# A two-layer graph kernel: counting steps, zeroing, the split of x and two orders of work are changed together

## The chip, the cores and the metric

One Trainium2 chip, one NeuronCore. The time is the device time of the whole program in microseconds (us). A run gives one time; the figure before is the median of three runs.

## The reference

A graph of 6,250 nodes with 256 features and 100,000 edges sorted by their target. Two layers, each a sum over incoming edges, then two dense products; at the end the input is added and every row is normalised:

```python
def _gin_agg(h, src, dst, eps, n_nodes):
    agg = jax.ops.segment_sum(h[src], dst, num_segments=n_nodes)
    return (1.0 + eps) * h + agg
...
h = _gin_agg(x, src, dst, eps1, n)
h = jax.nn.relu(h @ W1a + b1a)          # 256 -> 512
h = jax.nn.relu(h @ W1b + b1b)          # 512 -> 512
h = _gin_agg(h, src, dst, eps2, n)
h = jax.nn.relu(h @ W2a + b2a)          # 512 -> 512
out = h @ W2b + b2b                     # 512 -> 256
...
x = _layernorm(x + out)
```

The targets are drawn as 6250 u², so the first nodes have very many edges and the last ones few.

## The kernel before

Nodes stand in 49 tiles of 128 rows, edges in 782 chunks of 128. The program runs in three parts: a preparation (edge lists are turned and verified; the result is a flag), layer 1 and layer 2. A set flag sends the program into a slow general path; here it isn't set.

**Two ways of summing.** The edges of the first tiles (tiles 0 to 9 in layer 1, 340 chunks) are *counted*: for every pair of target and source the kernel counts how many edges there are, and the sum over edges becomes a dense product of the matrix of counts with all of x. The other chunks are *gathered*: POOL fetches 128 source rows per chunk by an indirect DMA (L504), and TensorE sums them with a selection matrix (`sums`, L1211; `merge`, L1256; VectorE adds into the tile's accumulator, L1268).

**Counting** (`counting`, `counted_`; layer 1 only). For each chunk VectorE makes `ca`, a one-hot matrix of the low seven bits of the source (L1883; one instruction makes four chunks), and `cb`, a one-hot row of the tile and the target's place in a window of w nodes (L1893). TensorE multiplies them (L1936, `ca` is stationary). 245 *steps* of one to eight chunks run from the last counted chunk down: 31 of one chunk and w = 11, which take two PSUM banks each; 149 of one chunk and w = 7 to 10; 65 of more chunks. After a step ScalarE copies the first w − 1 columns into the 8-bit table `at` (or the 16-bit `at_first`) at a place that a register holds (L1977), and VectorE adds the last column to what stands there (L1985). Before the first such copy both tables are zeroed by ScalarE (`zeroing`, L1912). A step needs a *permit* from a room of `SIDE` = 3 before it asks for its banks, and gives it back after the addition. Steps of one chunk with w ≤ 10 are started two at a time, and such a pair needs both its permits first.

**Products of counts with x** (`first_products`). x is loaded in ranges of four tiles into one buffer `raw`, split into an upper and a lower part (`splitting`, L1696 to L1699), stored as `halves`, and multiplied with the counts in three passes over all 49 tiles (`PASSES`: tiles 9 and 8, tiles 7 to 4, tiles 3 to 0; L1752 converts counts, L1811 multiplies). The first pass takes the split tiles as they come; the others load `halves` again. A pass starts when its tiles have been counted.

**The dense part** (`dense`): transposes (L1334), the first product (L1383), ScalarE's relu (L1393), the second product (L1412), and in layer 1 a store of the result h (L1426).

**Layer 2** gathers rows of h, so its gathers start after the last store of layer 1. Its counted tiles 0 to 7 use the counts kept in DRAM: `second_products` goes over 13 ranges of four tiles from the last to the first (`rs`; the last range, 12, is one tile of 106 rows), with two buffers for rows of h (`xr`, `upper`) and two for each kind of counts (`ci`). For the first two ranges of that order the rows are loaded and halved at the end of layer 1 (`sooner`, `SOONER` = 2).

**The order of work** on each engine is written out by a planner (`Plan`) when the program is built: it runs all of these as processes over rooms of buffers (eight PSUM banks among them) with estimated costs; counting steps ask for TensorE with priority 0, like sums, dense work with 2. On the chip each engine follows its list in order and waits on semaphores.

## Time and profile before

| | us |
|---|---|
| median of three runs | 1537.58 |
| lowest and highest | 1535.27, 1547.84 |
| the profiled execution's own time | 1526.32 |
| its span from the first to the last instruction | 1524.6 |
| mean granted TensorE clock (share of full speed) | 0.935 |
| TensorE busy | 1297.8 (85%) |
| VectorE, ScalarE, POOL busy | 811.6, 618.4, 895.2 |

Preparation ends at about 28 us, layer 1 at about 746 us. A share of busy time is over the whole span; what an edit is worth has to be read in the stretch in which it lies. Instructions are named by engine (PE is TensorE, PEld its weight loads, DVE VectorE, ACT ScalarE, SP the queue that issues most DMAs) and by the line of the kernel.

### The profile page before, as it was taken

The page shows a single profiled execution, that of the slowest core. Times are in us where ns is not written, and L with a number is a line of the kernel's source. Part 1 is how long each engine was busy: PE and PEld are TensorE (multiplying, and loading weights), DVE is VectorE, ACT ScalarE, POOL GpSimd, SP SyncE. Part 2 cuts the span into 40 slices and gives each one's busy share as a digit, 9 for nine tenths or more (in the row PEclk, how much of TensorE's full clock was granted, in tenths as well). Part 3 has the DMA queues.
Part 4 walks back from the last instruction along what each step waited for, and adds up shares of the span by engine and source line. Part 5 has one row for each costly group of instructions (what it writes and reads, how often), then busy time and mean ns, then how long its engine had stood idle before and what let it go on. Part 6 is the DMA issues. An engine that isn't in the chain of part 4 may idle for free.

```text
span 1524.6 us, 20531 instructions
## 1 busy us (share of the span) xinstructions
PE 1297.8 (85%) x6367; PEld 820.3 (54%) x6367; DVE 811.6 (53%) x2122; ACT 618.4 (41%) x1293; POOL 895.2 (59%) x944
## 2 busy tenths in 40 slices
PE   3478978879888899889968999997989999979997
PEld 2135545436554445555545666665556665656665
DVE  5575756655567883113146665764455544534343
ACT  3656556545555434444533423323233323321211
POOL 7565665565666766661256656664666666656640
PEclk7589988989999999999989999999999999999999
DMA  4555666647774436893478767776677877767650
GB/s 122 163 168 177 221 210 201 204 126 228 235 229 127 119 117 197 272 288 106 160 253 303 228 199 255 225 217 213 210 238 245 259 235 234 221 178 210 199 163 27
DMA packets 154445, 304.29 MB, mean 200 GB/s; under 512 B 34606, under 2 KB 69254, under 8 KB 154328
## 3 DMA queue, kind: packets, MB, share of 16 engines
q0 software_dynamic: 59136, 182.25, 39.6%
q1 hardware_dynamic: 87716, 107.04, 21.6%
q10 hardware_dynamic: 7476, 13.60, 2.5%
q8 instruction: 54, 0.88, 0.2%
q14 instruction: 63, 0.52, 0.1%
HBM read 263.18 MB, written 39.63 MB: 199 GB/s over the span
## 4 chain that ended last, share of the span: by engine, by line
PE 69%; DVE 9%; issue 8%; another core or an unknown queue 4%; ACT 4%; DMA 2%; POOL 1%; DVEq 1%; ACTq 1%; SPq 0%; POOLq 0%
PE bank L1383 17%; PE bank L1412 15%; PE bank L1211 11%; PE bank L1648 9%; PE bank L1811 7%; PE bank L1936 4%; PE bank L1256 4%; PE bank L1334 2%; DVE at L1985 1%; DVE cb L1893 1%; DVE acc L1591 1%; DVE acc L1268 1%; DMA xh<-halves 1%; DVE sel L1160 1%
## 5 line engine op out<-in xcount | busy, mean ns | idle before, releaser
L504 POOL DMA_INDIRECT early<-in_x_dram,srcs x442 | 435.9, 986 | 256.4 <-issue 113.0
L504 POOL DMA_INDIRECT early<-h,srcs x238 | 229.7, 965 | 186.5 <-issue 61.5
L504 POOL DMA_INDIRECT late<-h,srcs x236 | 227.2, 963 | 139.8 <-issue 59.1
L1268 DVE SCALAR_TENSOR_TENSOR acc<-bank,mask,acc 128x512 f32<-128x512 f32 (+1 forms) x365 | 210.9, 611 | 80.0 <-PE bank L1256 21.4
L1383 PE MATMUL bank<-zt,wide_w 128*128 128x256 f32 (+2 forms) x832 | 191.4, 387 | 24.5 <-ACT zt L1355 15.3
L1412 PE MATMUL bank<-wide_w,ht 128*128 128x512 f32 (+1 forms) x392 | 188.5, 607 | 3.2 <-DVE xh L1699 3.2
L1383 PEld LDWEIGHTS bank<-zt,wide_w 128*128 128x128 f32 x832 | 159.6, 203 | 55.6 <-ACT zt L1355 17.4
L1211 PE MATMUL bank<-early,sel 128*32 128x256 f32 (+1 forms) x1360 | 157.4, 489 | 30.2 <-issue 20.3
L1648 PE MATMUL bank<-upper,cfs 128*128 128x512 f32 (+1 forms) x392 | 169.4, 432 | 14.6 <-issue 10.9
L1811 PE MATMUL bank<-cf,xh 128*128 128x512 f32 (+2 forms) x588 | 150.2, 389 | 17.1 <-ACT cf L1752 10.2
L1648 PE MATMUL bank<-xr,cfs 128*128 128x512 f32 (+1 forms) x392 | 155.5, 397 | 0.0
L1977 ACT CAST at<-bank 128x250 f32 (+4 forms) x238 | 113.9, 494 | 99.7 <-PE bank L1936 32.6
L1575 ACT CAST cfs<-ci 128x512 fp32r<-128x512 uint8 (+3 forms) x104 | 60.7, 595 | 220.8 <-PE bank L1648 80.1
L1936 PE MATMUL bank<-cb,ca 128*128 128x490 f16 (+7 forms) x371 | 96.2, 340 | 58.6 <-DVE cb L1893 20.0
L1591 DVE TENSOR_TENSOR acc<-bank,acc 128x512 f32<-128x512 f32 x96 | 65.3, 684 | 137.9 <-remote 50.0
L1160 DVE TENSOR_TENSOR sel<-iota,slot 128x256 f32<-128x256 f32 (+3 forms) x109 | 47.6, 436 | 164.8 <-PE bank L1211 122.2
L1811 PEld LDWEIGHTS bank<-cf,xh 128*128 128x128 f32 (+1 forms) x588 | 100.8, 196 | 50.5 <-issue 20.7
L1256 PE MATMUL bank<-split,to 128*128 128x512 f32 (+3 forms) x306 | 89.8, 398 | 38.7 <-DVE split L1246 19.4
L1893 DVE TENSOR_SCALAR cb<-numbers,spot 128x492 f16<-128x492 f16 (+7 forms) x340 | 99.8, 330 | 40.0 <-remote 12.1
L1383 PE MATMUL bank<-zt,narrow_w 128*128 128x256 f32 (+2 forms) x432 | 103.3, 387 | 6.5 <-issue 4.0
L1211 PEld LDWEIGHTS bank<-early,sel 128*32 128x32 f32 x1360 | 40.0, 112 | 127.0 <-issue 107.0
L1412 PEld LDWEIGHTS bank<-wide_w,ht 128*128 128x128 f32 (+1 forms) x392 | 71.2, 193 | 66.7 <-issue 59.6
(150 smaller groups left out, 1702.4 us busy)
## 6 DMA issues: line engine op xcount, KB each, us to landing
xh<-halves SPq DMA_DIRECT2D x48, 512.0 KB
halves<-xh SPq DMA_DIRECT2D x24, 512.0 KB
h<-h1r ACTq DMA_DIRECT2D x48, 256.0 KB
xr<-h SPq DMA_DIRECT2D x12, 1024.0 KB
acc<-h SPq DMA_DIRECT2D x18, 512.0 KB
early<-in_x_dram,srcs POOLq DMA_INDIRECT x442
raw<-in_x_dram SPq DMA_DIRECT2D x12, 512.0 KB
r<-in_x_dram SPq DMA_DIRECT2D x22, 256.0 KB
```

The costliest lines, as they stand in the source:

```text
L504: nc.gpsimd.indirect_dma_start(out=rows_[:, j, :], out_offset=None, in_=table, in_offset=bass.IndirectOffsetOnAxis(ap=srcs[:, c : c + 1], ...
L1211: mm = nc.tensor.matmul(pm[b * SLOTS : (b + 1) * SLOTS], sel[:, c - groups[g][0], :], rows_[:, l, :], start=(c == part[0]), stop=(c == par ...
L1256: nc.tensor.matmul(pu[:, i * width : (i + 1) * width], to[:used], split[:used, l, i * width : (i + 1) * width], start=(l == 0), stop=(l == 1),
L1268: nc.vector.scalar_tensor_tensor(acc[t], pu[:, i * width : (i + 1) * width], mask[:, t - lo[g], g : g + 1], acc[t], op0=ALU.mult, op1=ALU.add,
L1383: nc.tensor.matmul(ph[:, (f - o) * TILES * P : (f - o) * TILES * P + nb], wa[:, k, f * P : (f + 1) * P], zt[:, k, :nb], start=(k == 0), st ...
L1412: nc.tensor.matmul(po[:m], ht[:, f, i * P : i * P + m], wb[:, f, :], start=(f == 0), stop=(f == KH - 1),)
L1591: nc.vector.tensor_tensor(acc[t], bank[token.number][:, :width], acc[t], op=ALU.add)
L1648: nc.tensor.matmul(bank[token.number][:, :width], cf[:m, j, :], of[:m, j, :], start=(j == 0 and of is upper), stop=(j == len(ks) - 1 and o ...
L1811: nc.tensor.matmul(to[:, :c], of, factor, start=(k == 0 and l == 0), stop=last, skip_group_check=True,)
L1893: made = nc.vector.tensor_scalar(token.tile[:, :e], numbers[:, :e], spot[:, c : c + 1], None, op0=ALU.is_equal,)
L1936: mm = nc.tensor.matmul(bank[token[l].number][:, : (k1 - k0) * w], a.tile[:, c % BATCH, :], b.tile[:, k0 * w : k1 * w], start=(j == 0), st ...
L1977: nc.scalar.copy(of[:, k0:k1, UNDER - w + 1 :][:, :, bass.ds(v, w - 1)], ap[:, :, : w - 1],)
```

## The change

- `SIDE` is 4 instead of 3. 
- Zeroing covers only the columns of `at` below the places of the smallest counted targets and above those of the largest (72 and 212 of 1188 bytes per tile, by the constants of the program), and `at_first` as before. The preparation verifies in addition, span by span of steps (`apart`), that each step's window reaches the one before it; one verification over 340 columns shrinks to 8.
- `ca` is laid out with four chunks interleaved: the element of chunk c and column j stands at 4j + c. It is made from a 16-bit copy of the column numbers (`rows_of_`, made once), so both inputs and the output have 16 bits. TensorE's stationary operand is read with a step of four elements.
- x is loaded and split in pairs of tiles with two buffers instead of ranges of four with one, and begins by the planner's clock at 50 instead of 60 us. The small integers of the start use a buffer of `ht` instead of the one of `raw`.
- In layer 1 the last two groups of gathered chunks change places, and the tiles that the last four groups (was three) touch are dense blocks of their own.
- In layer 2 the one-tile range 12 comes last instead of first; so ranges 11 and 10 are the two that are prepared at the end of layer 1.

The diff, cut to its core:

```diff
-SIDE = 3
+SIDE = 4
+SPLIT = 50.0
+RAWS = 2
-ENDING = 3
+ENDING = (4, 3)
...
+        down = list(reversed(range(BEGIN[number - 1], NG)))
+        if number == 1:
+            down[-2:] = reversed(down[-2:])
...
+        before_ = prep.tile([P, NC], F32, name="before_")
+        nc.scalar.copy(before_, cp)
...
-        violated(compare, NC, near, wide_of, op=ALU.is_ge)
+        violated(compare, taken[0][2], near[:, : taken[0][2]], wide_of[:, : taken[0][2]], op=ALU.is_ge)
...
+        def apart(v):
+            for a, b, n, w in taken:
+                if a:
+                    add_compare(
+                        v[:, a - least_n : a - least_n + n], cp[:, a : a + n], -float(w),
+                        before_[:, a - 1 : a].to_broadcast([P, n]), op0=ALU.add, op1=ALU.is_ge,
+                    )
+                if b - a > n:
+                    add_compare(
+                        v[:, a + n - least_n : b - least_n], cp[:, a + n : b], -float(w),
+                        before_[:, a : b - n], op0=ALU.add, op1=ALU.is_ge,
+                    )
...
+        violated(apart, NC - least_n)
...
+        range_order = [*reversed(range(len(ranges) - 1)), len(ranges) - 1]
...
-                raw_room = Tiles(loan, [P, RANGE, width], F32, "raw", 1)
-                scratch = raw_room.take()
+                raw_room = Tiles(loan, [P, PAIR, width], F32, "raw", RAWS)
+                scratch = ht_room.take()
...
-                rs = list(reversed(range(len(ranges))))
+                rs = range_order
...
-                    yield ("rest", 60.0)
-                    for r, ks in enumerate(ranges):
+                    yield ("rest", SPLIT)
+                    landed = []
+                    for q, ks in enumerate(spans):
                         raw = yield ("get", raw_room, 0)
                         in_rows(ks, raw.tile, table)
-                        yield ("rest", LOAD)
-                        for o in range(0, len(ks), PAIR):
-                            two = ks[o : o + PAIR]
...
+                        landed.append(Event(plan))
+                        plan.at(plan.now + LOAD, landed[q].set)
+                        plan.start(parting(q, ks, raw, landed))
+
+                def parting(q, ks, raw, landed):
+                    yield ("until", landed[q])
+                    if q:
+                        yield ("until", parted[q - 1])
...
-                    for i, r in enumerate(reversed(range(len(ranges) - SOONER, len(ranges)))):
+                    for i, r in enumerate(range_order[:SOONER]):
...
-                ca_room = Tiles(loan, [P, BATCH, P], F16, "ca", 4)
+                ca_room = Tiles(loan, [P, P, BATCH], F16, "ca", 4)
+                rows_of_ = loan.tile([P, P, BATCH], F16, name="rows_of_")
...
+                    nc.vector.tensor_copy(
+                        rows_of_, numbers[:, :P].unsqueeze(2).to_broadcast([P, P, BATCH])
+                    )
...
                                 nc.vector.tensor_tensor(
-                                    token.tile[:, :n, :],
-                                    line.unsqueeze(1).to_broadcast([P, n, P]),
-                                    low[:, q * BATCH : q * BATCH + n].unsqueeze(2).to_broadcast(
-                                        [P, n, P]
+                                    token.tile[:, :, :n], rows_of_[:, :, :n],
+                                    low[:, q * BATCH : q * BATCH + n].unsqueeze(1).to_broadcast(
+                                        [P, P, n]
                                     ),
                                     op=ALU.is_equal,
                                 )
...
-                    for k, (of, i, n) in enumerate(
-                        [(at, i, 7) for i in range(0, NT, 7)] + [(at_first, 0, NT)]
-                    ):
-                        some = of[:, i : i + n, :].rearrange("p a b -> p (a b)")
+                    over = (LOW[STEPS[0][0]] - BASE + UNDER) // 4 * 4
+                    under = -(-(HIGH[FINE] - BASE + UNDER + 1) // 4) * 4
+                    for some in (at[:, :, over:], at[:, :, :under], at_first):
                         some = some.bitcast(F32)
...
-                                    a.tile[:, c % BATCH, :], b.tile[:, k0 * w : k1 * w],
+                                    a.tile[:, :, c % BATCH], b.tile[:, k0 * w : k1 * w],
```

## Rows read from the trace of the kernel before

**Rows 1.** First line of the page: span and number of instructions.
```profile
span 1524.6 us, 20531 instructions
```
**Rows 2.** Windows: stretch, length, busy us and instructions per engine, clock, DMA share, GB/s.
```profile
60.00:110.00 50.00, 33.79 (x164) 16.40 (x163) 35.78 (x123) 27.72 (x77) 30.04 (x32) 0.74 0.45 139
110.00:350.00 240.00, 197.48 (x997) 115.69 (x997) 153.97 (x402) 136.09 (x283) 141.87 (x145) 0.90 0.61 190
350.00:600.00 250.00, 221.31 (x1126) 124.85 (x1126) 162.63 (x494) 120.30 (x256) 162.42 (x163) 0.98 0.57 174
600.00:746.00 146.00, 133.80 (x643) 79.45 (x641) 32.13 (x66) 59.46 (x157) 62.26 (x66) 0.99 0.65 208
776.00:1506.00 730.00, 661.28 (x3212) 451.29 (x3213) 386.98 (x770) 228.78 (x446) 435.99 (x452) 0.96 0.70 219
```
**Rows 3.** Windows of the counting matmuls L1936 alone: PE, PEld, clock, DMA, GB/s.
```profile
60.00:110.00 50.00, 14.02 (x56) 5.62 (x55) 0.74 0.45 139
...
120.00:450.00 330.00, 43.79 (x148) 11.49 (x149) 0.93 0.66 205
450.00:580.00 130.00, 34.74 (x159) 13.89 (x157) 0.99 0.41 124
```
**Rows 4.** Timeline (start, us, engine, line), one counting pair and the next.
```profile
206.78 0.59 PE L1936 MATMUL bank<-cb,ca 128*128 128x490 f16 x2
207.19 1.21 ACT L1977 CAST at<-bank 128x441 f32 x2 [0.41 <-PE bank L1936]
208.44 0.84 DVE L1985 TENSOR_TENSOR at<-bank,at 128x49 f32 x2 [0.48 <-issue]
210.53 0.59 PE L1936 MATMUL bank<-cb,ca 128*128 128x490 f16 x2
```
**Rows 5.** Groups of zeroing (busy, mean ns, idle before), then timeline: the first copies of counts.
```profile
L1912 ACT COPY at<-zero 128x2079 f32<-128x2079 f32 x7 | 13.3, 1914 | 0.0
L1912 ACT COPY at_first<-zero 128x3381 f32<-128x3381 f32 x1 | 3.0, 3014 | 0.0
...
58.62 1.64 ACT L1977 CAST at<-bank 128x250 f32 x5
```
**Rows 6.** Groups of VectorE in 110 to 350 us: those of counting.
```profile
L1985 DVE TENSOR_TENSOR at<-bank,at 128x49 f32 (+1 forms) x102 | 36.5, 361 | 14.2 <-issue 5.5 <-ACT at L1977 4.5 <-DVE at L1985 0.5
L1893 DVE TENSOR_SCALAR cb<-numbers,spot 128x492 f16<-128x492 f16 (+2 forms) x99 | 31.4, 351 | 14.6 <-PE bank L1936 5.0 <-remote 4.1 <-PE bank L1412 3.8
L1883 DVE TENSOR_TENSOR ca<-iota,low 128x512 f16<-128x512 f32 x25 | 17.2, 687 | 0.5 <-issue 0.3
```
**Rows 7.** Groups of TensorE, shapes apart: two weight loads, two moving operands of the preparation.
```profile
L1811 PEld LDWEIGHTS bank<-cf,xh 128*128 128x128 f32 x576 | 98.8, 196 | 50.2 <-issue 20.7 <-ACT cf L1752 14.6 <-ACT ht L1393 0.6
...
L1936 PEld LDWEIGHTS <-ca 128*128 128x128 f16 x371 | 32.3, 102 | 119.8 <-issue 65.9 <-DVE cb L1893 30.8 <-DVE at L1985 8.1
...
L687 PE MATMUL cp<-dstf,last 128*128 128x104 f32 x2 | 0.7, 471 | 0.0
L712 PE MATMUL heads<-dstf,first 128*128 128x96 f32 x2 | 0.7, 462 | 0.0
```
**Rows 8.** Tile raw: the split's copies, ns min/median/max, first and last start.
```profile
L1696 ACT CAST xh<-raw x25: 395/619/641, 89.9 to 292.5; 128x512 fp32r<-128x512 f32 x24, 106x256 fp32r<-106x256 f32 x1
```
**Rows 9.** Window of L1648 alone at the start of layer 2; timeline of three engines after it.
```profile
746.00:753.70 7.70, 5.53 (x16) 2.88 (x17) 1.00 0.54 168
...
776.00 0.80 PE L1648 MATMUL bank<-upper,cfs 128*128 128x512 f32 x1 [10.32 <-issue]
...
775.33 0.62 ACT L1575 CAST cfs<-ci 128x512 fp32r<-128x512 uint8 x1 [12.04 <-remote]
...
775.35 0.69 DVE L1591 TENSOR_TENSOR acc<-bank,acc 128x512 f32<-128x512 f32 x1 [11.96 <-remote]
```
**Rows 10.** Groups of VectorE in the preparation: the flag's sum, a short verification.
```profile
L834 DVE TENSOR_REDUCE fsum<-fp 1x1 f32<-1x473 f32 x1 | 0.6, 636 | 7.6 <-remote 7.6
...
L759 DVE TENSOR_TENSOR viol<-cp,dstf 128x4 f16<-128x4 f32 x2 | 0.3, 152 | 0.0
```

80 lines of the change are left out of this document (44 added, 36 removed).

## The prediction

> **What bounds the kernel now.** I read windows cut where the work changes, then the counting's own windows and one pair's timeline, then the groups that each edit touches. The windows first [rows 2]. TensorE is what all else feeds, but not equally: from 776 to 1506 us it is busy 661 of 730 us at a clock of 0.96, from 600 to 746 us 134 of 146 us, from 350 to 600 us 221 of 250 us at 0.98. From 60 to 350 us it is busy only 33.8 + 197.5 = 231 of 290 us, and at a granted clock of 0.74 and then 0.90; the clock has two levels, 1.2 and 2.4 GHz, so 0.90 means that a fifth of the stretch ran at the lower one. That early stretch has the time to be won; later TensorE is full.
>
> Why is it underfed? The windows of the counting matmuls alone give 148 matmuls, 74 pairs, in the 330 us from 120 to 450 us [rows 3]: 4.46 us a pair. The timeline of one pair shows a strict chain [rows 4]: two matmuls at 206.78, ScalarE's two copies at 207.19, VectorE's additions at 208.44 to 209.28, and only then, at 210.53, the next pair's matmuls. That follows from the code: a pair needs two permits, there are three, so one pair is under way. Counting ends only at about 580 us, and the last pass of products can start no earlier.
>
> **Four permits.** They let two pairs run at once. The floor by the chain is half of 4.46, 2.23 us a pair. The floor by VectorE: a pair costs 2 × 0.361 + 2 × 0.351 us and half of one `ca` instruction, 0.34 us [rows 6], in all 1.77 us; other work takes 154 − 85 = 69 of VectorE's 240 us there [rows 2, 6], so at most 71% is free, 2.5 us a pair. I take 3.2 us, a little nearer that floor than today's 4.46: 74 × 1.26 = 93 us less counting, its end near 490 us instead of 580. Counting then gates nothing that TensorE could not fill otherwise, so the gain is not 93 us but what TensorE's idle and slow time in 60 to 350 us gives back. Work in full-clock time: 33.8 × 0.74 + 197.5 × 0.90 = 203 us. From 350 to 600 us, where there is much to choose from, the yield is 221.3 × 0.98 / 250 = 0.867 [rows 2]. At that yield 203 us would need 234 us, 56 us less than 290. This is the far end. The near end is nothing: the two permits more hold two more of eight PSUM banks, and the first pass holds two, so less is left for sums and dense blocks. I take half, **−28 us**.
>
> **The split of x in pairs.** Its 25 copies run from 89.9 to 292.5 us [rows 8], 8.4 us apart, because one buffer is loaded, split twice and only then loaded again. Two buffers overlap load and split; the first pass can then end tens of us earlier and gives TensorE more to do in the same poor stretch. It is one of the means to the −28, not a term beside it. The earlier start competes on SP's queue with loads of weights and accumulators; today's first split is at 89.9 us [rows 8], far behind its 60, so other things hold it there; I cost the earlier start at nothing, and at 1 to 2 us if it delays a weight. ScalarE, VectorE and stores have the same count as before.
>
> **Few zeros.** Zeroing now costs 7 × 1.914 + 3.014 = 16.4 us of ScalarE [rows 5]. The two rows give 0.845 ns an element and 0.157 us fixed. 49 × 53 and 49 × 18 elements cost 2.35 and 0.90 us by that, with the unchanged 3.01 us 6.3 us in all: 10.1 us less. It lies on a path: the first copy of counts starts at 58.62 us, right behind the last zeros. Rows of 53 words with gaps may cost more than one run; no row shows it, and twice the price still saves 7 us. A counting chain that starts 10 us sooner counts only if it stays the gate, and with four permits it does not; I put it at 0 in the sum and −10 as its far end.
>
> **`ca` in 16 bits.** VectorE's 0.687 us is between two bounds: no gain, and the 0.351 us of the 16-bit `cb` of nearly the same length [rows 6]. I take 0.43 us, nearer to `cb`, as all operands now have its width: 85 × 0.26 = 22 us of VectorE saved, plus one instruction of 0.35 to 0.7 us for `rows_of_`. VectorE is busy 64% from 110 to 350 us [rows 2], so this is no term either, but lowers its floor for a pair from 2.5 to 2.3 us. The Trainium skill, "VectorE: DVE Perf Modes", section on the perf-mode tier table, gives two-input instructions twice the rate when everything is 16 bits wide and none of the fourfold rate of one-input ones; no row here shows such an instruction. By it the estimate would be 0.687 less 256 elements at 0.96 GHz, 0.42 us, and the sum is the same.
>
> **The interleaved weight load.** 371 loads of 0.102 us become loads with a step of 8 bytes. Nothing in the trace has such a stationary operand. The nearest: a moving operand with a step of 8 bytes, 96 columns in 462 ns, beside 104 columns, each value read again and again, in 471 ns [rows 7], so the step costs nothing there. At the other end stands the 0.196 us load of 32-bit operands: 371 × 0.094 = 35 us if none of it is hidden. Loads run beside the matmul before them (16.4 us of loads in a stretch with 33.8 us of matmuls, [rows 2]), so even that would be partly covered. I take 0 by the nearer row, and keep +35. The Trainium skill, "SBUF — State Buffer", specifications, says that SBUF is read in lines of 16 bytes and that full rate wants at least two hits in a line; a step of 8 bytes gives just two, so it promises no loss, with no margin; no run here shows it yet.
>
> **The preparation.** About 32 short verifications more. One lasts 0.152 us [rows 10] and they overlap, so 3 to 5 us of VectorE, less 0.3 us for the shortened one, and one copy of 340 columns on ScalarE. VectorE then stands 7.6 us before the flag's sum [rows 10]: that hides them. Were the wait one that moves along, it would be +3 to +5 us.
>
> **The last groups swapped** changes which tiles end layer 1. From 600 us TensorE is full [rows 2], so the order inside is worth 0 to −2 us; I take 0.
>
> **Layer 2's order.** Today the one-tile range 12 comes first: from 746 to 753.7 us its 16 matmuls and what lies between them fill the time, though the modelled busy time is 5.5 us [rows 9]; they are held up by ScalarE's conversions and first copies, which serve one tile where they could serve four. In the new order that start-up lies beside range 11's four times longer work, and range 12 costs its few us later, among work that fills TensorE: I take **−4 us**. Behind it stands a hole of 10.3 us up to 776.00 us [rows 9], and one might count it as the price of loading range 10 late. I don't: ScalarE and VectorE wake within 0.02 us of each other at 775.33 and 775.35 us, both marked "remote", a release that the profile can't place, and what they then do belongs to range 11, which was loaded. If the hole goes with the order after all, it is 10 us more; if the larger start makes another, 10 us less than nothing: −14 to +6 for this edit. Behind it TensorE is busy nine tenths of the time [rows 2], so a shift here reaches the end.
>
> **Sum.** −28 − 4 = −32 us. Against the profiled execution: its own 1526.3 us (span 1524.6 [rows 1] and 1.7 around it) becomes 1494. The median of the runs shown is 11.3 us above that execution, and it is the median that is forecast: 1537.6 − 32 = 1506 us.
>
> **Rivals.**
> 1. *Layer 1 gains nothing.* Counting ends sooner, but TensorE's early idle time only changes its cause: dense work waits for banks instead of counts. For it: four wide steps hold eight banks of eight, four narrow ones and the first pass six. Against it: banks are also held for a shorter time in all. Layer 2's start still gains: 1537.6 − 4 = 1534 us.
> 2. *Bank shortage makes it slower.* In the 31 wide steps sums get a bank only between steps; the 50 us up to 110 us hold 33.8 us of matmuls, of which 14.0 are counting [rows 2, 3], so up to 20 us of other work slide; and if the yield from 110 to 350 us falls from 197.5 to 180 of 240 us, 17 us more: 37 − 4 − 10 for the early start = +23, 1561 us. It decides once TensorE is busy under about 0.75 of that stretch, against 0.82 now. Against it: the planner gives sums the first free bank.
> 3. *The stepped weight load costs as much as a 32-bit one*, +35 and unhidden: 1541 us, no change. Speaks for it: no row shows such a load; against it, the moving operand.
> A `ca` instruction that does not get faster takes the 22 us of VectorE back; then the floor stays 2.5 us a pair and the forecast hardly moves.
>
> **How the numbers follow.** Forecast 0.64, rival 1 0.19, rival 2 0.10, rival 3 0.07 (spread evenly over the three signs). About 1%, 15 us, is what a measurement tells from no change. Faster by over 1%: 0.64 + 0.02 = 0.66; within 1%: 0.19 + 0.03 = 0.22; slower: 0.10 + 0.02 = 0.12. The forecast alone runs from −62 (nine tenths of the 56, and −12 at layer 2's start) to −16: 1476 to 1522. With rival 1 and rival 3 the range goes to 1545; below 1475 and above 1545 stay about 2 in 10.
>
> **What would show it.** Right: counting pairs of L1936 overlap, near 3 us apart, its last matmul before 520 us; clock over 0.95 and TensorE busy over 0.86 from 110 to 350 us; first L1977 near 48 us; `ca` near 0.43 us; weight loads of L1936 near 0.10 us; layer 1 ends near 718 us. Whether the hole of 10 us is still there tells what it was. Wrong: counting ends early and layer 1 still ends near 746 us (rival 1), L1211 waits for banks and POOL with it before 110 us (rival 2), PEld of L1936 near 0.2 us (rival 3).

## The result, and the profile after

The changed kernel is slower: a median of 1548.0 us against 1530.8 us of the kernel before, 15 runs each, a ratio of 1.013 (95% interval 1.011 to 1.016). The forecast was 1506 us, 0.979 of the 1537.6 us known when it was made. The profiled execution of the changed kernel took 1553.6 us, that of before 1526.3 us, so these two are 27 us apart where the medians are 17 apart. Line numbers moved: L1936 is L1977 now, L1977 is L2018, L1211 is L1244, L504 is L516, L834 is L863, L1575 is L1608, L1591 is L1624.

First line of the page, then windows of the changed kernel in the columns of [rows 2]; the last is layer 2, moved by the 9 us by which it begins later:

```profile
span 1551.6 us, 20503 instructions
```

```profile
60.00:110.00 50.00, 27.35 (x136) 14.30 (x135) 30.73 (x103) 23.19 (x64) 27.85 (x30) 0.61 0.40 119
110.00:350.00 240.00, 200.06 (x1029) 118.18 (x1022) 161.23 (x451) 147.62 (x311) 140.25 (x147) 0.93 0.63 199
350.00:600.00 250.00, 225.41 (x1140) 135.01 (x1139) 136.80 (x446) 120.26 (x275) 155.01 (x162) 0.97 0.64 197
600.00:746.00 146.00, 134.11 (x624) 73.81 (x624) 39.38 (x79) 50.58 (x119) 75.72 (x79) 0.96 0.55 175
785.00:1515.00 730.00, 645.14 (x3071) 430.65 (x3074) 379.12 (x748) 221.60 (x434) 432.28 (x452) 0.95 0.70 218
```

From 110 to 600 us TensorE does a little more than before [rows 2]. The loss stands at both ends: from 60 to 110 us it is busy 27.4 us where it was 33.8, at a clock of 0.61 where it was 0.74, and in the 730 us of layer 2 it is busy 645 us where it was 661. Three instructions date it. The first group's selection, right behind the flag, starts at 42.8 us where it was 28.4:

```profile
41.87 0.14 DVE L864 CAST flag<-fsum 1x1 int32<-1x1 f32 x1
42.78 0.36 DVE L1193 TENSOR_TENSOR sel<-iota,slot 128x192 f32<-128x192 f32 x1 [0.76 <-DVE flag L864]
```

Layer 2's first conversion starts at 754.9 us where it was 745.9, and the span ends at 1551.6 us where it ended at 1524.6 [rows 1]. So the preparation grew by 14.4 us, layer 1 (selection to conversion) fell from 717.5 to 712.1 us, and layer 2 grew from 778.7 to 796.7 us: 14.4 − 5.4 + 18.0 = 27.0.

These are one execution of each kernel. In layer 2 all kernels below that share an order of ranges run the same instructions in the same order on TensorE, ScalarE and GpSimd; where the kernel before takes 1526 to 1532 us, their layer 2 took 774.8 to 785.2 us with the old order (790.7 in e5) and 788.3 to 796.7 with the new one. So some of the 18.0 us are chance.

Windows of the counting matmuls alone, as in [rows 3]: none starts behind 520 us, where 159 stood from 450 to 580 us before. Counting does end early, and layer 1 does not.

```profile
60.00:110.00 50.00, 13.12 (x48) 5.14 (x47) 0.61 0.40 119
118.00:382.00 264.00, 41.19 (x134) 13.25 (x134) 0.93 0.66 207
450.00:520.00 70.00, 18.69 (x96) 9.72 (x95) 0.98 0.38 115
520.00:600.00 80.00, 0.00 (x0) 0.00 (x0) 0.96 0.79 240
```

### The profile page after: what moved, and what is told of

Its sections match the earlier page's. It is cut to its first block, busy times and chain, and to the rows that moved or that the text cites. A ratio compares the mean times of both kernels' runs of the same rounds, so it can differ in the third digit from the quotient of the medians.

```text
span 1551.6 us, 20503 instructions
## 1 busy us (share of the span) xinstructions
PE 1309.9 (84%) x6364; PEld 824.1 (53%) x6364; DVE 798.6 (51%) x2155; ACT 607.5 (39%) x1289; POOL 879.8 (57%) x944
## 3 DMA queue, kind: packets, MB, share of 16 engines
q1 hardware_dynamic: 87908, 107.04, 21.3%
## 4 chain that ended last, share of the span: by engine, by line
PE 64%; DVE 13%; another core or an unknown queue 9%; issue 8%; ACT 4%; DVEq 1%; DMA 0%; ACTq 0%
PE bank L1416 15%; PE bank L1445 14%; PE bank L1244 10%; PE bank L1681 9%; PE bank L1851 7%; PE bank L1289 3%; PE bank L1977 3%; DVE acc L1301 2%; PE bank L1367 1%; DVE at L2026 1%; DVE cb L1937 1%; ACT at L2018 1%; DVE acc L1624 1%; DVE split L1279 1%
## 5 line engine op out<-in xcount | busy, mean ns | idle before, releaser
L516 POOL DMA_INDIRECT early<-in_x_dram,srcs x442 | 424.3, 960 | 287.1 <-issue 112.3
L516 POOL DMA_INDIRECT early<-h,srcs x238 | 228.1, 959 | 188.3 <-issue 62.1
L516 POOL DMA_INDIRECT late<-h,srcs x236 | 224.9, 953 | 153.7 <-PE bank L1244 65.9
L1445 PE MATMUL bank<-wide_w,ht 128*128 128x512 f32 (+1 forms) x392 | 193.4, 622 | 1.1 <-DVE cb L1937 0.6
L1244 PE MATMUL bank<-early,sel 128*32 128x256 f32 (+1 forms) x1360 | 158.7, 489 | 33.3 <-issue 11.6
L1624 DVE TENSOR_TENSOR acc<-bank,acc 128x512 f32<-128x512 f32 x96 | 65.5, 685 | 195.2 <-remote 56.9
L2018 ACT CAST at<-bank 128x250 f32 (+4 forms) x238 | 114.1, 495 | 105.2 <-PE bank L1977 34.6
L1608 ACT CAST cfs<-ci 128x512 fp32r<-128x512 uint8 (+3 forms) x104 | 61.2, 594 | 228.5 <-remote 79.1
L1977 PE MATMUL bank<-cb,ca 128*128 128x490 f16 (+7 forms) x371 | 96.7, 347 | 51.2 <-DVE at L2026 15.1
L1289 PE MATMUL bank<-split,to 128*128 128x512 f32 (+3 forms) x306 | 86.5, 390 | 35.2 <-DVE split L1279 10.5
L1244 PEld LDWEIGHTS bank<-early,sel 128*32 128x32 f32 x1360 | 38.0, 112 | 134.6 <-issue 97.5
```

The source lines that it names most:

```text
L516: nc.gpsimd.indirect_dma_start(out=rows_[:, j, :], out_offset=None, in_=table, in_offset=bass.IndirectOffsetOnAxis(ap=srcs[:, c : c + 1], ...
L1244: mm = nc.tensor.matmul(pm[b * SLOTS : (b + 1) * SLOTS], sel[:, c - groups[g][0], :], rows_[:, l, :], start=(c == part[0]), stop=(c == par ...
L1289: nc.tensor.matmul(pu[:, i * width : (i + 1) * width], to[:used], split[:used, l, i * width : (i + 1) * width], start=(l == 0), stop=(l == 1),
L1445: nc.tensor.matmul(po[:m], ht[:, f, i * P : i * P + m], wb[:, f, :], start=(f == 0), stop=(f == KH - 1),)
L1624: nc.vector.tensor_tensor(acc[t], bank[token.number][:, :width], acc[t], op=ALU.add)
L1977: mm = nc.tensor.matmul(bank[token[l].number][:, : (k1 - k0) * w], a.tile[:, :, c % BATCH], b.tile[:, k0 * w : k1 * w], start=(j == 0), st ...
```

## The experiments

Each ratio is to the kernel before, run beside it on the same chip. That kernel took 1526 to 1532 us beside the first eight experiments and the f runs, but 1559 to 1564 us beside e9 to e12 and the g runs, so across sets only ratios are compared. The sets (e1 to e4, e5 to e8, e9 to e12, f, g) ran on five chips, and the changed kernel was not measured on the slower ones: that a ratio holds on another chip is assumed, not shown. e5 rests on four runs, the others on eight or more. "Layer 1's end" is the start of layer 2's first conversion.

| run | what differs | ratio | 95% interval |
|---|---|---|---|
| changed kernel | | 1.0131 | 1.0106 to 1.0155 |
| e1 | before + verifications | 1.0046 | 1.0008 to 1.0084 |
| e2 | changed − verifications | 1.0083 | 1.0045 to 1.0122 |
| e3 | changed, gathers held | 1.0095 | 1.0058 to 1.0133 |
| e4 | changed, old order of ranges | 1.0046 | 1.0014 to 1.0078 |
| e5 | before + fourth permit | 1.0181 | 1.0124 to 1.0238 |
| e6 | before, gathers held | 1.0049 | 1.0013 to 1.0086 |
| e7 | before, layer 2's gathers held | 0.9974 | 0.9935 to 1.0012 |
| e8 | changed, held, old order | 1.0030 | 0.9993 to 1.0067 |
| e9 | changed, three permits | 0.9985 | 0.9952 to 1.0019 |
| e10 | changed, held, old order, three permits | 0.9962 | 0.9936 to 0.9989 |
| e11 | e10 with layer 2's gathers held | 0.9952 | 0.9924 to 0.9981 |
| e12 | before + new order | 1.0069 | 1.0034 to 1.0104 |
| f1 | before, fourth permit late | 0.9998 | 0.9967 to 1.0028 |
| f2 | e8, fourth permit late | 1.0030 | 1.0001 to 1.0059 |
| f3 | before + 16-bit `ca` | 1.0026 | 0.9994 to 1.0058 |
| f4 | before + x in pairs | 1.0063 | 1.0020 to 1.0106 |
| g1 | before + few zeros | 1.0012 | 0.9977 to 1.0046 |
| g2 | before + few zeros, verifications, held, swap | 1.0016 | 0.9978 to 1.0055 |

### The start: verifications beside a burst of gathers

The timeline of VectorE in the changed kernel (start, busy us, idle before) shows that the verifications are short and far apart:

```profile
12.68 0.16 DVE L792 SCALAR_TENSOR_TENSOR viol<-cp,before__331 128x8 f16<-128x8 f32 x1
...
18.18 0.16 DVE L787 SCALAR_TENSOR_TENSOR viol<-cp,before__331 128x2 f16<-128x2 f32 x1 [0.53 <-issue]
18.87 0.18 DVE L792 SCALAR_TENSOR_TENSOR viol<-cp,before__331 128x16 f16<-128x16 f32 x1 [0.54 <-issue]
...
35.02 0.19 DVE L792 SCALAR_TENSOR_TENSOR viol<-cp,before__331 128x30 f16<-128x30 f32 x1 [1.23 <-issue]
```

0.16 to 0.19 us busy, but each starts 0.70 us or twice that behind the last, with no wait that the profile shows ("issue"). Four experiments (e1, e2, e3, e6) ask what the start costs.

**e1**, the verifications added to the kernel before:

```diff
+        before_ = prep.tile([P, NC], F32, name="before_")
+        nc.scalar.copy(before_, cp)
-        violated(compare, NC, near, wide_of, op=ALU.is_ge)
+        violated(compare, taken[0][2], near[:, : taken[0][2]], wide_of[:, : taken[0][2]], op=ALU.is_ge)
+        violated(apart, NC - least_n)
```

> The kernel before with one part of the change alone: the 32 new short verifications (and the copy of the counts that they read, and the shortened one). Theory 1, the start: in the trace of the changed kernel the first group's selection begins at 42.8 us instead of 28.4, because these verifications run about 0.7 us apart from 12.7 to 35.7 us, and 14 us later at the start is 14 us later at the end, since TensorE has no slack behind it. Then this kernel is 10 to 15 us slower than the kernel before, about 1.0065 to 1.01 of it, and its selection begins near 42 us. Theory 2, the start is absorbed and layer 2's new order of ranges is what costs: then this kernel is within 3 us of the kernel before, though it too begins late.

Measured: 1.0046 (1.0008 to 1.0084), less than theory 1 gave, and not nothing. The selection starts at 42.1 us, as in the changed kernel; yet the profiled layer 1 ends at 746.4 us, where it ended at 745.9. The old layer 1 makes the late start good.

How late the verifications make the flag is less sure than the two traces say. With the old preparation it comes at 24.1 to 29.0 us in before, e2, e5, e7 and f4, but at 37.3 to 38.1 us in e12, f1, f3 and g1, whose preparation is the same:

```profile
37.26 0.14 DVE L835 CAST flag<-fsum 1x1 int32<-1x1 f32 x1
```

That is f1. With the new verifications it comes at 41.0 to 42.0 us (changed kernel, e1, e4, e9). So they cost between 3 and 18 us of the start, not 14.

**e2**, the changed kernel without them:

```diff
-        violated(apart, NC - least_n)
-        violated(compare, taken[0][2], near[:, : taken[0][2]], wide_of[:, : taken[0][2]], op=ALU.is_ge)
+        violated(compare, NC, near, wide_of, op=ALU.is_ge)
```

> The changed kernel without the new verifications (their copy gone too, the shortened verification long again, so part of what the change verifies is left out; the computed result is the same). Theory 1, the start: its selection begins near 28 us as before, and it is 12 to 15 us faster than the changed kernel, near 1534 us, that is 1.000 to 1.004 of the kernel before. Theory 2, layer 2's order: under 4 us faster than the changed kernel, 1.010 or more of the kernel before.

Measured: 1.0083, 0.5% under the changed kernel (the two intervals overlap): both theories had too sharp an edge, and the truth lies between. Selection at 25.0 us, layer 1's end at 741.4 instead of 754.9 us.

**e3**, the changed kernel with 16 of the 22 gathers that open layer 1 behind the flag (the expectation counts 24; six stay ahead, not eight):

```diff
-        for i in range(EARLY, PIECES):
-            gathered[i] = gather(1, i, x, D, early)
...
-        nc.vector.tensor_copy(flag, fsum)
+        flagged = nc.vector.tensor_copy(flag, fsum)
+        for i in range(EARLY, PIECES):
+            gathered[i] = gather(1, i, x, D, early)
+            if i == EARLY:
+                together(gathered[i][1][0], [flagged])
```

> The changed kernel, all of it, but the 16 gathers that stand ahead of the flag are issued behind it: only the first 8 run beside the verifications. Theory 3, the burst: VectorE's new verifications are not long in themselves (0.15 to 0.2 us busy each); they are 0.7 us apart while GpSimd issues gathers one behind the other, and the pace ends within 2 to 4 us of the last gather. Then they run about 0.07 us apart once the first gathers are out, the selection begins near 20 to 24 us, and the kernel is 12 to 20 us faster than the changed kernel, 1528 to 1536 us, though 16 gathers start later. Theory 4, the verifications are slow by their own nature (short instructions on one row of counts): they stay 0.7 us apart, the selection begins near 43 us again, and with the gathers behind it the kernel is 0 to 10 us slower than the changed kernel.

Measured: the mechanism as theory 3 said, the time only in part. Groups of VectorE from 12 to 43 us in the changed kernel (busy us, mean ns, idle before), and the same from 12 to 23 us in e3:

```profile
L792 DVE SCALAR_TENSOR_TENSOR viol<-cp,before__331 128x16 f16<-128x16 f32 (+8 forms) x15 | 2.7, 177 | 9.4 <-issue 9.4
L787 DVE SCALAR_TENSOR_TENSOR viol<-cp,before__331 128x2 f16<-128x2 f32 (+3 forms) x17 | 2.5, 158 | 8.5 <-issue 8.5
```

```profile
L787 DVE SCALAR_TENSOR_TENSOR viol<-cp,before__331 128x2 f16<-128x2 f32 (+3 forms) x17 | 2.3, 147 | 0.0
L792 DVE SCALAR_TENSOR_TENSOR viol<-cp,before__331 128x16 f16<-128x16 f32 (+8 forms) x15 | 2.3, 164 | 0.0
...
21.33 0.14 DVE L862 CAST flag<-fsum 1x1 int32<-1x1 f32 x1
```

The same 32 instructions have 17.9 us of idle time before them beside the gathers and none without; the flag comes at 21.3 us instead of 41.9. But 20 us sooner are worth only 0.4% over all runs (1.0095, with intervals that overlap), a third of what I expected. The one profiled execution says more, layer 1's end at 741.5 us and a span 22 us shorter than the changed kernel's: one execution is not the median, and a few us of it are not evidence.

**e6**, the same hold in the kernel before (same edit):

> The kernel before with 16 of the 24 gathers ahead of the flag issued behind it, as in the third experiment. Theory 3, the burst: the wait of 7.6 us before the flag's sum goes, the selection begins near 20 to 21 us instead of 28.4. What that is worth: the first experiment began 14 us later and ended layer 1 at the same 746 us, so an earlier start should be worth little here, 0 to 6 us faster (0.996 to 1.000). If the start bounded layer 1 it would be 8 us faster.

Measured: 1.0049, a miss. The selection starts at 20.2 us, 8 us sooner, layer 1 ends at 743.8 us, and the kernel is half a per cent slower. With e1, which starts 14 us later and is also half a per cent slower, this says that in the kernel before the time of the start is not handed on to the end. Behind the selection, TensorE, VectorE and ScalarE run the same instructions in the same order in layer 1 of before, e1 and e6, so another order is not the reason; whether a mere shift in time costs half a per cent, or chance does, is not shown. In the changed kernel, whose lists e2 and e3 share, an earlier start is handed on in part: their traces end layer 1 13 us sooner. Differences of half a per cent I read with care, or not at all.

### Layer 2's order of ranges

**e4**, the changed kernel with the old order:

```diff
-        range_order = [*reversed(range(len(ranges) - 1)), len(ranges) - 1]
+        range_order = list(reversed(range(len(ranges))))
```

> The changed kernel with layer 2's ranges in the old order (the range of one tile first). Theory 2, layer 2's order: layer 2 takes 791 us in the trace of the changed kernel and 774 before, with a wait of 33 us of VectorE's first additions at its start and 12 us more of TensorE's idle time; then this kernel is 10 to 17 us faster than the changed kernel, near 1531 to 1538 us. Theory 1, the start: the order is worth less than 4 us either way, and it stays near 1548 us.

**e12**, the new order in the kernel before (`rs = range_order` in the products, `range_order[:SOONER]` in the early loads, as in the change):

> The kernel before with layer 2's new order of ranges alone. The forecast's step: 4 us faster (6 slower to 14 faster), as the start-up lies beside the four tiles of range 11. Theory 2: 8 to 17 us slower, 1.005 to 1.011, because the small range's buffers no longer come free at 754 us for the load of the third range: the first additions of VectorE start 30 us later than in the kernel before, and TensorE's idle time grows between 50 and 100 and between 200 and 250 us of layer 2.

Measured: 1.0046, that is 0.85% or 13 us under the changed kernel, and 1.0069, 11 us over the kernel before. Both as theory 2 said. The timeline shows the difference at the start: VectorE's first addition and SyncE's load of the third range, first in the changed kernel, then in e4, whose layer 2 begins at 760.3 us.

```profile
788.67 0.69 DVE L1624 TENSOR_TENSOR acc<-bank,acc 128x512 f32<-128x512 f32 x1 [32.89 <-issue]
...
788.48 0.37 SPq L896 DMA_DIRECT2D xr<-h  x1
```

```profile
770.37 0.69 DVE L1624 TENSOR_TENSOR acc<-bank,acc 128x512 f32<-128x512 f32 x1 [9.23 <-issue]
...
768.25 0.37 SPq L896 DMA_DIRECT2D xr<-h  x1
```

Two ranges are loaded ahead, and the third waits for the first one's buffer. The old first range is one tile, done 8 us after layer 2's start (754.0 us before, 768.3 in e4); the new one is four tiles, done after 34 us (788.5 us, and 797.3 in e12, which begins at 763.3). Windows of the changed kernel, from 50 to 100 and from 650 to 750 us of layer 2, then the same of e4:

```profile
805.00:855.00 50.00, 36.99 (x165) 23.32 (x164) 30.90 (x51) 14.14 (x26) 28.69 (x31) 0.90 0.84 281
...
1405.00:1505.00 100.00, 84.02 (x393) 57.61 (x394) 30.75 (x73) 18.26 (x42) 50.94 (x55) 0.90 0.55 164
```

```profile
810.00:860.00 50.00, 43.91 (x220) 30.37 (x220) 35.40 (x61) 22.74 (x43) 31.27 (x32) 0.93 0.80 274
...
1410.00:1510.00 100.00, 93.53 (x482) 66.10 (x482) 37.69 (x88) 20.56 (x48) 53.94 (x56) 0.97 0.59 180
```

TensorE does 7 us less behind the late load and 9.5 us less in the last stretch. The first of the two is chance: e8 has the old order and does as little from 50 to 100 us of its layer 2.

```profile
798.00:848.00 50.00, 37.25 (x173) 25.43 (x172) 30.09 (x52) 19.20 (x37) 29.41 (x30) 0.86 0.78 269
```

Over all twenty profiled executions that stretch holds 35.4 to 43.9 us with the old order (15) and 37.0 to 41.9 us with the new one (5). From 650 to 750 us they part: 90.3 to 93.9 us with the old order, 80.2 to 86.5 with the new; from 300 to 350 us the new order wins some back (43.3 to 48.2 against 37.5 to 41.3). So the order costs 0.7 to 0.85%, and it shows at the end of layer 2. The late load is seen; how it, or the small range at the end, makes that loss is not shown.

**e7**, the kernel before with layer 2's opening gathers (22, not 24 as the expectation has it) in parts:

```diff
-                for i in range(PIECES):
+                for i in range(2):
                     fetch_rows(i)
+                def more():
+                    for i in range(2, PIECES):
+                        if not i % 2:
+                            yield ("rest", 16.0)
+                        fetch_rows(i)
+                        if not i % 2:
+                            together(gathered[i][1][0], latest)
+                plan.start(more())
```

(`latest` is the product written last.)

> The kernel before; of the 24 gathers that open layer 2 only 8 are issued at once, the next 8 and the last 8 each wait for products about 16 us apart. Theory 3, the burst: the hole of 10.3 us of TensorE before 776 us ends where the 22 gathers in a row end (775.8 us; 776.2 and 778.6 in the first experiment, 784.6 and 789 in the changed kernel), because matmuls that are ready are held up behind them; then the hole shrinks to under 4 us, the products of the second range run on from 766 us, and the kernel is 4 to 10 us faster than before (0.993 to 0.997). Theory 6, the hole is a late load of the third range: it stays near 10 us at the same place, and the kernel is 0 to 6 us slower, as gathers come later.

Inconclusive: 0.9974 (0.9935 to 1.0012), and the burst was not broken. GpSimd still issued 22 gathers in a row, from 743.0 to 770.2 us. The window of e7 in which TensorE stands still lies inside it:

```profile
760.00:770.00 10.00, 0.00 (x0) 0.00 (x0) 0.17 (x1) 0.19 (x1) 7.56 (x9) 0.71 0.76 229
770.00:794.00 24.00, 21.43 (x82) 13.83 (x83) 14.25 (x23) 11.36 (x21) 10.80 (x12) 0.84 0.70 242
```

**e8**, held gathers and old order together in the changed kernel (the edits of e3 and e4):

> The changed kernel with two things put right: 16 gathers behind the flag (third experiment) and layer 2's ranges in the old order (fourth). If start and order are all that the change lost, and their costs add (5 and 13 us of 20), it stands within 0.3% of the kernel before, 0.997 to 1.003: the rest of the change (four permits, x in pairs, few zeros, the 16-bit operands, the swapped groups) then brings nothing that can be measured. If the rest is worth what the forecast said, it is 0.98 to 0.99.

Measured: 1.0030 (0.9993 to 1.0067), as the first reading said: what is left of the change, the fourth permit included, is worth nothing that shows.

### The fourth permit

**e5**, before with one number changed:

```diff
-SIDE = 3
+SIDE = 4
```

> The kernel before with one number changed: four permits for the counting steps instead of three. The forecast's step (four permits are worth about 28 us of layer 1): counting ends near 500 us instead of 579, TensorE is busier from 60 to 350 us, and the kernel is 15 to 28 us faster, 0.982 to 0.990 of the kernel before. Theory 5, the stream of sums: layer 1's end stands 50 us behind its last gather whatever the counting does (694 and 746 us before, 713 and 755 in the changed kernel), and the fourth permit only lets counts go ahead of sums from 60 to 130 us: the 40th gather starts later than 62 us (80 in the changed kernel, 72 with its start put right), counting ends near 510 us, and the kernel is within 1% of the kernel before, rather 2 to 8 us slower than faster.

Measured: 1.0181 (1.0124 to 1.0238). Counting ends at 533 us instead of 579, and the kernel is 28 us slower, more than theory 5 dared. Layer 1 ends at 765.9 us, 20 us later than before; the other 12 us of the difference of the two traces lie in layer 2, whose lists are unchanged, and have no cause that I can name. GpSimd's gathers from 40 to 130 us (count, busy us, mean ns, idle time before them and its releasers) show it; before, changed kernel, e5, f1:

```profile
L504 POOL DMA_INDIRECT early<-in_x_dram,srcs x56 | 55.4, 989 | 36.2 <-issue 13.5 <-PE bank L1211 11.4 <-PE bank L1936 5.4
```

```profile
L516 POOL DMA_INDIRECT early<-in_x_dram,srcs x48 | 46.3, 964 | 51.7 <-PE bank L1244 28.9 <-issue 11.9 <-PE bank L1977 5.3
```

```profile
L504 POOL DMA_INDIRECT early<-in_x_dram,srcs x45 | 44.2, 982 | 52.6 <-PE bank L1211 32.0 <-issue 10.4 <-PE bank L1936 6.1
```

```profile
L504 POOL DMA_INDIRECT early<-in_x_dram,srcs x58 | 57.0, 982 | 40.8 <-PE bank L1211 18.3 <-issue 13.1 <-PE bank L1936 7.8
```

Gathers wait for sums (L1211, L1244 now) to free their rows, and that wait grows from 11.4 to 32.0 us with the fourth permit. In e5 the 41st gather (the one that the expectations call the 40th) starts at 83 us instead of 62 and the last at 719 instead of 694; layer 1 ends 47 to 52 us behind the last gather in both.

TensorE's timeline behind the selection shows what the sums wait for; before, e5, changed kernel:

```profile
28.91 1.92 PE L1211 MATMUL bank<-early,sel 128*32 128x256 f32 x12 [11.09 <-issue]
44.08 1.08 PE L1936 MATMUL bank<-cb,ca 128*128 128x275 f16 x4 [13.26 <-DVE cb L1893]
```

```profile
39.28 1.98 PE L1936 MATMUL bank<-cb,ca 128*128 128x275 f16 x8 [21.36 <-DVE cb L1893]
55.66 1.07 PE L1211 MATMUL bank<-early,sel 128*32 128x256 f32 x4 [14.40 <-DVE at L1985]
```

```profile
50.74 1.99 PE L1977 MATMUL bank<-cb,ca 128*128 128x275 f16 x8 [10.10 <-DVE cb L1937]
52.96 1.92 PE L1244 MATMUL bank<-early,sel 128*32 128x256 f32 x12 [0.23 <-DVE at L2026]
```

Before, the first sums run 0.46 us behind the selection, and counting comes after them. With four permits from the start, the eight matmuls of four wide steps stand ahead of the first sum in TensorE's list and fill all eight banks; the first sum waits until VectorE's first addition gives a bank back. In e5 that addition waits for the end of the zeros (the first copy of counts starts at 54.4 us), and the first sum starts 25.8 us behind the selection. In the changed kernel it is 10.2 us. All six kernels with four permits from the start show this (10.1 to 25.8 us); in the other fourteen, f1 and f2 among them, it is 0.46 us. The zeros make it worse: TensorE stands idle ahead of that first sum for 14.4 us in e5, and for 0.1 to 3.5 us in the five kernels with few zeros. Of the 28.9 us in the changed kernel, 21.6 us are one wait up to 54.3 us, and part of it is the late flag: e1, as late but with three permits, waits 11.1 us there.

**e9**, the changed kernel with three permits (`SIDE = 3`):

> The changed kernel with three permits for counting again, all else of the change kept. Theory 7, the fourth permit takes banks from the sums: alone on the kernel before it cost 1.8% (fifth experiment), with the 40th gather at 83 us instead of 62 and layer 1's end at 766 instead of 746. Then here the 40th gather comes 5 to 15 us sooner than the 80 us of the changed kernel, layer 1 ends 8 to 20 us sooner than 755, and the kernel is 0.5 to 1.3% faster than the changed kernel, 1.000 to 1.008 of the kernel before. If the permit only did harm in the kernel before (its one buffer for x, its long zeros), the time stays that of the changed kernel, 1.011 to 1.015.

Measured: 0.9985 (0.9952 to 1.0019), by the ratios 1.5% under the changed kernel (which was measured on another, faster chip), more than expected. 56 gathers start from 40 to 130 us again, and their wait for sums is 17.4 us.

**f1**, before, with four permits of which one is held back until the 31 wide steps are counted:

```diff
+            def fourth():
+                token = yield ("get", permits, 0)
+                yield ("until", counted_to[sum(len(parts_of(w)) > 1 for _, _, w in STEPS) - 1])
+                token.release()
...
+                plan.start(fourth())
                 plan.start(counting())
```

> The kernel before with four permits, but the fourth is given only when the 31 wide counting steps (two banks each) are done. Theory 7, banks in the wide steps: three of them hold six banks of eight as in the kernel before, so the 40th gather starts near 62 to 68 us again, not at 83 as with four from the start; counting still ends before 579 us, and the kernel is between 5 us faster and 5 us slower than before (0.997 to 1.003). Theory 8, counts that are ahead take TensorE's time from sums wherever they stand: gathers fall back behind the wide steps too, and the kernel stays over 1% slower.

Measured: 0.9998 (0.9967 to 1.0028). Counting ends at 524 us, 54 us sooner than before, 58 gathers fall from 40 to 130 us (above), and the time is that of before. So theory 7 holds in the kernel before: the price comes with the fourth permit in the wide steps, where e5's trace shows the banks held. And counting that ends 54 us sooner is worth nothing by itself.

**f2**, the kernel of e8 with the same late fourth permit:

> The changed kernel with layer 2's old order, 16 gathers behind the flag, and its fourth permit only behind the wide steps. With four from the start this kernel stood at 1.003 of the kernel before (eighth experiment), with three throughout at 0.996 (tenth). Theory 7: 0.993 to 0.998, no worse than with three. Theory 8: 1.000 to 1.005.

Measured: 1.0030 (1.0001 to 1.0059), theory 7 missed here: the late permit is no better than four from the start. With its selection at 22 us, e8 had its 41st gather at 73 us and f2 at 72, so there was little to win in the wide steps, though f2's first sum again starts 0.46 us behind the selection and e8's 10.9 us. The result lies in theory 8's range. Whether a permit behind the wide steps costs something in this kernel, against the 0.996 of three permits measured on another chip (e10), is open.

### The other parts, and what is left

**e10**, the changed kernel with three permits, old order and held gathers (the edits of e9, e4, e3):

> The changed kernel with the three things that the runs so far named put right: three permits, layer 2's old order, 16 gathers behind the flag. What is left of the change is x in pairs, few zeros with their verifications, the 16-bit operands and the swapped groups. Theory 7 (permit 8 to 20 us): 0.985 to 0.997 of the kernel before, as the eighth experiment without the first of the three stands at 1.003. If the permit is worth nothing here: 1.000 to 1.006.

Measured: 0.9962 (0.9936 to 0.9989), the upper end of what theory 7 gave: a little faster than the kernel before, and by the ratios than the changed one. But beside e9, on the same chip, order and held gathers together are worth 0.2%, where e4 and e3 gave them 1.2%.

**e11**, with e7's edit besides:

> As the kernel beside it, and with layer 2's opening gathers in three parts, as in the seventh experiment (there 0.997, 0.9935 to 1.0012). If the hole at layer 2's start goes here too, 3 to 8 us faster than the kernel beside it; if that gain was chance, the same as it.

Measured: 0.9952 (0.9924 to 0.9981): not to be told from e10. It is the lowest ratio measured, by the ratios about 1.8% under the changed kernel.

**f3**, before with 16-bit interleaved `ca`:

```diff
-                ca_room = Tiles(loan, [P, BATCH, P], F16, "ca", 4)
+                ca_room = Tiles(loan, [P, P, BATCH], F16, "ca", 4)
...
-                                    a.tile[:, c % BATCH, :], b.tile[:, k0 * w : k1 * w],
+                                    a.tile[:, :, c % BATCH], b.tile[:, k0 * w : k1 * w],
```

> The kernel before with the stationary operands of counting made four chunks interleaved in 16 bits, and nothing else. The forecast's steps: 0.43 us instead of 0.69 for each of the 85 instructions, 0.10 us still for each of the 371 weight loads, and no difference in time (0.997 to 1.003). The forecast's third rival, the load with a step of 8 bytes costs as much as a 32-bit one: weight loads near 0.2 us and up to 35 us slower, 1.01 to 1.023.

Measured: 1.0026 (0.9994 to 1.0058), no difference shown. Its groups (busy us, mean ns, idle before):

```profile
L1940 PEld LDWEIGHTS <-ca 128*128 128x128 f16 x371 | 37.5, 119 | 105.9 <-issue 63.3 <-DVE cb L1897 15.5 <-DVE at L1989 12.8
L1888 DVE TENSOR_TENSOR ca<-rows_of__522,low 128x512 f16<-128x512 f16 x85 | 37.1, 437 | 2.0 <-issue 1.7
```

**f4**, before with x split in pairs from two buffers:

```diff
-                raw_room = Tiles(loan, [P, RANGE, width], F32, "raw", 1)
-                scratch = raw_room.take()
+                raw_room = Tiles(loan, [P, PAIR, width], F32, "raw", RAWS)
+                scratch = ht_room.take()
```

> The kernel before with x split in pairs of tiles from two buffers, and nothing else. The 25 copies run from 90 to 293 us before and from 96 to about 250 us in the changed kernel. If the first pass of products was held up by them, TensorE gets work earlier and layer 1 ends 3 to 10 us sooner (0.994 to 0.998). If layer 1 hangs on its stream of sums alone, no difference (0.998 to 1.002).

Measured: 1.0063 (1.0020 to 1.0106), a miss on the other side. The copies end at 230 us instead of 292, and the kernel is slower; why is not settled.

**g1**, before with few zeros (the new `zeroing` of the change, nothing else):

> The kernel before with few zeros alone, without the verifications that go with them (so cells between counted windows are not verified to be covered; the result is the same). The forecast's step: ScalarE's zeroing falls from 16.4 to 6.3 us, the first copy of counts starts near 48 us instead of 58.6, and nothing of it reaches the end (0.998 to 1.002); its far end was 10 us (0.993). If the zeros are the part that pays for the others in the sum, 0.985 to 0.995, because the six banks of the first counting steps come free 10 us sooner, in the stretch where sums wait for banks.

Measured: 1.0012 (0.9977 to 1.0046), the forecast's nothing.

**g2**, the parts that had not lost alone (few zeros with verifications, held gathers, swapped groups, on the kernel before):

> The kernel before with what is left of the change when every part that lost alone is taken out: few zeros with their verifications, the swapped last groups, and 16 gathers behind the flag so that the verifications run unhindered. Three permits, x in fours, old operands, old order. The tenth experiment, which also had x in pairs and 16-bit operands, stood at 0.996. If the parts add, it is 0.985 to 0.992, the fastest so far; if what one part wins or loses depends on the plan that the others make, 0.994 to 1.002.

Measured: 1.0016 (0.9978 to 1.0055). The parts do not add. Taken alone they are +1.8 (permit), +0.7 (order), +0.6 (pairs), +0.5 (verifications), +0.3 (16 bits) and +0.1% (zeros), 4.0% together, and the change is +1.3%. e10 keeps pairs and 16 bits and stands lower than g2, which has neither, though on another chip and with intervals that overlap. The traces show which parts change the lists of work: verifications and held gathers leave those of TensorE, VectorE and ScalarE in layer 1 as they are; permit, pairs, zeros and 16 bits each give layer 1 another list, and only the order of ranges changes layer 2's. How zeros and permit act on each other is seen above. That other lists are why the rest doesn't add is argued, not shown.

## Why the prediction was wrong, point by point

- **Four permits, −28 us: the step that failed.** Its first half held. From the 66th counting matmul on, 144 of them (72 pairs) took 279 us instead of 329, 3.9 us a pair instead of 4.6, where the forecast put 3.2, and the last counting matmul started at 513 us, where I named 490 and a bound of 520. The second half, that TensorE would then fill its early idle time, was a yield (0.867 of full-clock time, that of 350 to 600 us) carried over from another stretch; from 110 to 350 us it rose only from 197.5 to 200.1 us at a clock of 0.93, where I had named 0.86 of the stretch and 0.95. f1 shows the gain of an early end of counting by itself: none. e5 shows the price, 1.8%, where the sum had nothing as its near end: the first sum stands 14.4 us for a bank, and starts 25.8 us behind the selection instead of 0.5.
- **Rival 2 was the right mechanism for the permit, and I gave it 0.10.** I wrote (under rival 1) that four wide steps hold all eight banks, that up to 20 us of other work slide before 110 us, and where to look: L1211 and with it POOL. That wait is what grew (11.4 to 28.9 us, of which the late flag has a part; 32.0 in e5, without it). Against it I held that the planner gives sums the first free bank; but in its list the first eight counting matmuls come ahead of the first sum. Its deciding sign, TensorE under 0.75 of 110 to 350 us, was put at the wrong place: it was 0.83 there, since most of the damage is done by 130 us and carried along: from the 41st to the last, gathers start 13 to 22 us later than before, 10 to 22 later than in e1, which starts as late.
- **The preparation, 0 (or +3 to 5): failed.** The count (32) and the length (0.15 us) were right. I took the wait of 7.6 us ahead of the flag's sum [rows 10] for free cover. It was marked "remote", and it goes when the gathers are held (e6); the same burst then held up most of the new instructions by 0.5 or 1.2 us: 17.9 us of idle time. In the two traces the flag comes 14 us later, but the old preparation alone moves it between 24 and 38 us. What reaches the end is about half a per cent (e1, e2).
- **Layer 2's order, −4 (−14 to +6): failed.** The gain at the start does not show: in the first 34 us of layer 2 TensorE is busy 20.6 to 22.0 us with the new order, 18.8 to 21.5 with the old. And the load of the third range waits for the first one's buffer, 34 us instead of 8. I had looked at that load as the reason for the hole of 10 us [rows 9] and, when it was not, dropped it. Measured +0.7 to +0.85% (e12, e4), 11 to 13 us; TensorE lacks them in the last stretch of layer 2, and how that follows is open.
- **The hole** was to tell by itself what it was. In the changed kernel TensorE stops at the same place for 4.9 and 7.7 us, up to 789 us, though ranges 11 and 10 are loaded ahead now. So it was not the load of range 10. In all the profiles, before and after among them, 22 gathers in a row open layer 2, and the hole ends between 3 us ahead and 5 us behind their end (775.8 us before, 770.2 in e7, 784.6 in the changed kernel, 779.5 in e11). But that burst always begins 2.5 us behind layer 2's start, so anything with a fixed delay would show the same, and e7 did not break it: that the burst makes the hole is likely by the start's example, and open.
- **Few zeros, 0: right for the part alone.** Zeroing takes 2.4 + 0.9 + 3.0 us, as worked out; g1 finds no difference. The first copy starts at 51.7 us, 8.9 us behind the selection instead of 30.2, but 14 us of that were lost ahead of it. What I missed is that they shorten the time for which four wide steps hold the banks.
- **`ca`, 0.43 us and 0 in the sum: right.** 427 ns. The Trainium skill, "VectorE: DVE Perf Modes", section on the perf-mode tier table, gave an estimate of 0.42 us by its doubled rate; the row agrees.
- **The weight load with a step of 8 bytes, 0: nearly right.** 119 ns instead of 102 [rows 7], 6 us in all, beside other matmuls; f3 shows no difference in time. The ten kernels with the step have 118.6 to 120.3 ns, the ten without 100.6 to 103.3. Rival 3 falls. The Trainium skill, "SBUF — State Buffer", Specifications, asks for at least two hits in a line of 16 bytes for the full rate; here two hits cost 17% more.
- **Pairs of x, a means to the −28:** earlier by 54 us at their end (238.9 us), and alone 0.6% slower.
- **The last groups swapped, 0:** not tried alone. From the last gather to layer 1's end it takes 40.0 to 44.7 us in the nine kernels built on the changed one and 47.0 to 55.6 us in the ten with the old ending, but 48.6 us in g2, which has the swap; so nothing is shown.

Rival 1 (layer 1 gains nothing, 1534 us) is what f1 shows for counting by itself. Put right for permits, order and gathers, the change ends at 0.996 (e10), near that rival's 0.998.

## What to carry to other kernels

Ask of a stage that you mean to speed up whether what comes behind it waits for it: here counting ended 54 us sooner for nothing, and layer 1's end stood 40 to 56 us behind its last gather in every kernel. A shared pool of buffers has its price at the moment when the widest users hold it, so look at who comes first in the list then; raising the limit once they are through cost nothing here (f1), and bought nothing. An unexplained wait is not free cover for new work until you know what makes it. And before you name a stretch of one trace as the place of a loss, look whether it keeps still in other runs with the same list of work.

## What the runs showed of the hardware that I had not expected

While GpSimd issued gathers one behind the other at the start (1.25 us each, 0.95 busy), other engines' instructions came 0.70 us or a multiple apart, from about 7 us behind its first gather on. In the changed kernel the burst's last gather starts at 31.8 us and VectorE's pace ends at 36.4 us; without the burst (e3) the same instructions run 0.07 us apart. SyncE shows it too. Its four short issues in a row under the burst in the kernel before, and the same four in the changed kernel behind it (start, us in all):

```profile
34.54 7.70 SPq L867 DMA_DIRECT2D acc<-in_x_dram  x4
```

```profile
43.33 1.60 SPq L896 DMA_DIRECT2D acc<-in_x_dram  x4
```

They take 6.3 to 8.4 us late in a burst (before, e2, e7, f4), 2.1 us at its end (e5) and 1.6 us in the fifteen other profiles.

The Trainium skill, "SBUF — State Buffer", section on the two separate sides, tells of VectorE holding up GpSimd's descriptors at their shared port. Here the direction is the other one, and SyncE is held up too, so that account does not explain it; what does, no run here shows.

So at the start of this kernel, gathers issued one behind the other were not free for the other engines.
